# A decoder layer on one core: 432 transfers of ScalarE's results issued from ScalarE's queue instead of SyncE's

## The chip, the core and the metric

The kernel runs on one core of a Trainium2 chip. The core has five engines with a queue of instructions each: TensorE (PE in the profile; its weight loads are PEld), VectorE (DVE), ScalarE (ACT), GpSimd (POOL) and SyncE (SP). SP does no arithmetic here: its queue only issues DMA transfers. Each queue is worked off in order, and a transfer can be issued from SP's, ACT's or POOL's. The metric is the device time of one execution in microseconds (us); shorter is better.

## What is computed

The reference is one decoder layer on x of shape 8 x 512 x 512 (batch, position, feature) in float32, with a context of the same shape:

```python
x = layernorm(x + mamba(x))                  # L0_attn
x = layernorm(x + attention(x, ctx, mask))   # L0_xattn, 16 heads of 32
x = layernorm(x + ffn(x))                    # 32 experts, 4 per token, plus a shared one
```

`mamba` normalizes x, projects it to 1024 inner channels and 1024 gates, convolves over 4 positions, and derives dt, B and C from the result (`x_dbl = x_main @ x_proj_w`, split into 32 + 16 + 16 columns). For each channel and each of 16 states it runs `h = exp(A*dt)*h + dt*B*x` along the positions and sums `h*C` over the states. `attention` is a softmax of q·k over 512 context positions. `ffn` picks four experts for each token by a gate, with a capacity of 640 tokens for each expert.

## The kernel before

The program has three functions in a row: `layers` (mamba, attention, the gate and the shared expert), `experts`, and `finish` (the last layer norm). The change touches `layers` alone.

`layers` handles 16 chunks of mamba: 8 batch elements in two chunks of 256 positions. Each chunk has 32 steps: 4 groups of 256 channels (q), 4 groups of states (g) and two halves (jj). In a step ACT makes four decays with `exp` (`decays`, L480) and copies the carried state into the head of a tile (`carry`, L488). DVE multiplies dt·x with B (`steps_in`, L494), runs the scan (L501) and multiplies with C (`collect`, L510). PE then sums over the states (L521). The decays have two buffers, so those of one step are written while the scan before runs.

While the mamba of batch element b runs, its steps are filled up with pieces of the attention of element b-1 and with the keys and values of element b (`sources`, `units`). The attention of the last element runs by itself after the last chunk. The work around the change is:

- **B and C.** `x_proj` makes dt, B and C on PE; `spill` copies them to `xd` on ACT (L406) and stores B and C to DRAM (L408). `bcast` (L418) reads them back, repeated over the partitions. Once for each chunk.
- **Values.** `values` projects the context on PE; `put` copies the rows to `v` on ACT (L721) and stores them (L722); `units` reads them back much later (L765). Four times for each batch element.
- **Maxima.** For a pair of heads, `maximum` computes scores on PE (L813), which DVE reduces to `mx` (L815). `negate` turns them around on PE (L822), ACT negates them into `nm` (L826), and two transfers put one row each into the query tile `qa` (L829). `weigh` (L839) multiplies keys with this tile, so that the scores come out less their maximum, and ACT takes `exp` of them (L843).
- **Result and sums.** `gather` (L855) multiplies the values with these exponentials. `split` copies the finished pair to `raw` on ACT (L867); four transfers put its halves into `attT` (L875) and the sums into `total` (L876). After two pairs, `divide` takes the reciprocal on ACT (L888, L889) and finishes it on DVE (L892 to L894). `total` has one buffer, so the next pair's sums can be written only when L894 has read it.

Further ACT operations on whose results DVE works at once are the chain of `prepare` (L447 to L453, then DVE L457 to L460), the first tap of the convolution (L369, then L377) and the roots of the layer norms (L68, L69, then L73).

SP's queue also issues all loads of weights and activations, the repeated dt and dt·x (`repeat`, L428) and the tiles of the attention (`spread`, L799 to L803). Two things set the order of a queue. The steps' code places a part of the side work in each third of a step and holds the second half of many a part back by three thirds (`wait`, `settle`). Then a planner, when the program is built, orders each engine's queue by when it expects an instruction to be ready: the order on an engine is not quite that of the source. Its waits follow from the data.

Of the kernel before, what the change touches and what calls it, by code (L numbers as in the profile page):

```python
# [17 lines left out]
P = 128  # L18
# [6 lines left out]
NST = 16  # L25
RANK = 32
# [10 lines left out]
HD = 32  # L37
# [51 lines left out]
def layers(ctx, tc, a, x1d, filld, based, xbuf):  # L89
# [23 lines left out]
    nc = tc.nc  # L113
# [23 lines left out]
    def rows(w):  # L137
        return w.rearrange("(c p) f -> p c f", p=P)
# [108 lines left out]
    def quad(tag, name):  # L247
        return big(tag, name)[:, 0 : DC * S].rearrange("p (c t) -> p c t", c=DC)
# [148 lines left out]
    def x_proj(f):  # L397
        psd = psm.tile([P, 2, T], F32, tag="mm", name="ps_d")
        for c in range(CC):
            nc.tensor.matmul(  # L400
                psd[0:64, 0, :], w_x[:, c, :], f["xs"][c // 2][:, c % 2, :], start=(c == 0), stop=(c == CC - 1)
            )

        def spill():
            f["xd"] = xd = mp.tile([64, T], F32, tag="xd", name="xd")
            nc.scalar.copy(xd, psd[0:64, 0, :])  # L406
            f["scr"] = scr = dp.tile([2 * NST, T], F32, tag="scr", name="scr")
            nc.sync.dma_start(scr, xd[RANK : RANK + 2 * NST, :])  # L408

        return spill  # L410

# [160 lines left out]
    def load(name):  # L572
        loaded[name] = w = p2.tile([P, DC, D], F32, tag="wa", name="wa")
        nc.sync.dma_start(w, rows(a[name]))
# [124 lines left out]
    kept = {}  # L699

    def sources(b):

        st, todo = {}, []

        def begin():
            load("Wv")
            st["cT"] = cT = quad("s2", "cT")
            nc.sync.dma_start(cT, rows(a["ctx"][b]))
            st["mk"] = mk = p1.tile([P, S], U8, tag="mk", name="mk")
            nc.sync.dma_start(mk, a["mask"][b : b + 1, :].to_broadcast([P, S]))  # L710
            kept[b] = [dp.tile([S, D], F32, tag="vd", name="vd"), dp.tile([D, S], F32, tag="kd", name="kd")]

        def values(pc):
            if pc == 0:
                load("Wk")
            w, cT = loaded["Wv"], st["cT"]
            ps = dense(lambda dc: cT[:, dc, pc * P : (pc + 1) * P], lambda dc: w[:, dc, :])

            def put():
                v = p3.tile([P, D], F32, tag="row", name="v")  # L720
                nc.scalar.copy(v, ps)  # L721
                nc.sync.dma_start(kept[b][0][pc * P : (pc + 1) * P, :], v)  # L722

            return put

        def keys(oc):
            if oc == 0 and b:
                load("Wq")
            w, cT = loaded["Wk"], st["cT"]
            ps = dense(lambda dc: w[:, dc, oc * P : (oc + 1) * P], lambda dc: cT[:, dc, :])  # L730

            def put():

                k = p3.tile([P, D], F32, tag="row", name="k")
                nc.vector.scalar_tensor_tensor(k, ps, bk[:, oc : oc + 1], st["mk"], ALU.add, ALU.mult)
                nc.sync.dma_start(kept[b][1][oc * P : (oc + 1) * P, :], k)

            return put

        todo.append((0, begin, False))  # L740
        for j in range(SC):
            todo.append((3.4, lambda j=j: values(j), False))
        for j in range(DC):
            todo.append((3.4, lambda j=j: keys(j), False))
        return todo

    def dense(lhs, rhs):
        ps = psm.tile([P, S], F32, tag="mm", name="ps_p")
        for dc in range(DC):
            nc.tensor.matmul(ps, lhs(dc), rhs(dc), start=(dc == 0), stop=(dc == DC - 1))  # L750
        return ps

    def units(b):

        st = {}
# [61 lines left out]
        def negate(i):  # L817

            mx = st.pop(("mx", i))
            pm = psm.tile([P, S], F32, tag="mm", name="ps_m")  # L820
            for lt in range(SC):
                nc.tensor.transpose(pm[0:2, lt * P : (lt + 1) * P], mx[:, lt, :], ident)  # L822

            def put():
                nm = p3.tile([P, D], F32, tag="row", name="nm")
                nc.scalar.mul(nm[0:2, :], pm[0:2, :], -1.0)  # L826
                for j in range(2):
                    r0 = j * 2 * HD + HD + 1
                    nc.sync.dma_start(st[i][0][r0 : r0 + 1, :], nm[j : j + 1, :])  # L829

            return put

# [14 lines left out]
        def gather(i, kc):  # L847

            if kc == 0:
                st["po"] = pso.tile([P, S], F32, tag="po", name="po")  # L850
                if i == 0:
                    st["attT"] = quad("s2", "attT")
            po, eT = st["po"], st.pop(("eT", i, kc))
            for j in range(2):
                nc.tensor.matmul(  # L855
                    po[j * 2 * HD : (j + 1) * 2 * HD, :],
                    va[:, kc, i, j * HD : (j + 2) * HD],
                    eT[:, j, :],
                    start=(kc == 0),
                    stop=(kc == SC - 1),  # L860
                )
            if kc < SC - 1:
                return

            def split():
                raw = p3.tile([P, D], F32, tag="row", name="raw")
                nc.scalar.copy(raw, po)  # L867
                if i % 2 == 0:
                    st["total"] = p1.tile([P, S], F32, tag="total", name="total")
                attT, total, oc = st["attT"], st["total"], i // 2  # L870
                for j in range(2):

                    r0, r1 = (0, HD) if j == 0 else (3 * HD, 2 * HD)
                    to = slice((i % 2) * 2 * HD + j * HD, (i % 2) * 2 * HD + (j + 1) * HD)
                    nc.sync.dma_start(attT[to, oc, :], raw[r0 : r0 + HD, :])  # L875
                    nc.sync.dma_start(total[to, :], raw[r1 : r1 + HD, :])  # L876

            return split

# [114 lines left out]
        for n in range(pairs * SC + 4):  # L994
            i, k = n // SC, n % SC
# [568 lines left out]
```

## Time and profile before

| | us |
|---|---|
| median of three runs (5405.52 to 5409.17) | 5408.32 |
| the profiled execution | 5406.28 |
| its span, first to last instruction | 5404.6 |
| PE busy | 4672.4 (86%) |
| DVE busy | 4235.9 (78%) |
| ACT busy | 2593.6 (48%) |
| stretch with mamba and attention together, 405 to 3515 us: PE / DVE / ACT busy | 2620.7 / 2836.3 / 1831.4 |
| the last attention by itself, 3515 to 3840 us: PE / DVE / ACT busy | 283.1 / 130.8 / 82.3 |
| experts and last norm, 3840 to 5404.6 us: PE / DVE / ACT busy | 1493.5 / 904.3 / 442.6 |

Times in the profile count from the span's start. "L480" is line 480 of the kernel. In a list of operations, `out<-in` names what is written and read, and "x4" counts instructions. Brackets give the idle time of the engine just before, and what ended it. In a list of waits, "DVE m L73 <- ACT r L69: 33.5, 26, 3.3" says that DVE's operation on line 73 stood waiting for ACT's line 69 for 33.5 us in total, 26 times, 3.3 us at the longest. "SPq" and "ACTq" mark instructions that only issue a transfer; they do not count as busy time. An operation's slack is the time between its end and the start of the operation that uses its result.

### The profile page before, as it was taken

To read this page: it belongs to the slowest core of one execution; us is meant where nothing else is said; L and a number is where in the kernel's file an instruction comes from. 1 tells how busy PE (TensorE), PEld (TensorE's weight loads), DVE (VectorE), ACT (ScalarE), POOL (GpSimd) and SP (SyncE) were. 2 spreads that over 40 slices of the span, in tenths; PEclk is the share of its full clock that TensorE was granted. 3 is DMA by queue.
4 is the path that set the end of the run, shared out by engine and by line. 5 is a ranking of instruction groups with operands and counts; after the bars stand their busy time and mean duration, and the time that the engine had idled before them with its cause. 6 is when DMAs were issued, how large, how long until landed. Compare 5 with 4: busy or idle time off the path is not lost. (4 is left out here: it accounts for less than half of the span.)

```text
span 5404.6 us, 53991 instructions
## 1 busy us (share of the span) xinstructions
PE 4672.4 (86%) x17320; PEld 2476.6 (46%) x17320; DVE 4235.9 (78%) x5369; ACT 2593.6 (48%) x5726; POOL 570.3 (11%) x426
## 2 busy tenths in 40 slices
PE   6768889788888988988888888789999999999994
PEld 3324234234333423433333342333677777777773
DVE  7999899989989989898998998943566555665554
ACT  5566565565656556566565655523222222222223
POOL 1000002002000200200200020011111111111111
PEclk8879989999999999999999999899999999999997
DMA  8875346345444634634544463342344444544544
GB/s 236 266 224 146 87 96 208 81 114 176 114 104 117 197 77 109 189 98 107 174 125 100 117 200 78 91 146 66 103 128 127 123 117 118 127 127 121 129 115 144
DMA packets 486427, 719.03 MB, mean 133 GB/s; under 512 B 117137, under 2 KB 200625, under 8 KB 484096
## 3 DMA queue, kind: packets, MB, share of 16 engines
q1 hardware_dynamic: 450128, 627.16, 41.1%
q0 software_dynamic: 33280, 76.90, 7.5%
q10 hardware_dynamic: 2736, 11.54, 0.5%
q8 instruction: 137, 2.24, 0.2%
q14 instruction: 146, 1.20, 0.1%
HBM read 391.24 MB, written 165.05 MB: 103 GB/s over the span
## 5 line engine op out<-in xcount | busy, mean ns | idle before, releaser
L480 ACT ACTIVATE l_da<-rep,l_aneg 128x256 f32<-128x256 f32 x2048 | 895.0, 501 | 941.8 <-DVE h L501 877.0
L501 DVE TENSOR_TENSOR_SCAN h<-l_da,h 128x1028 f32<-128x1028 f32 x512 | 1166.0, 2292 | 20.3 <-ACT l_da L480 17.7
L494 DVE TENSOR_TENSOR h<-rep,bc 128x1024 f32<-128x1024 f32 x512 | 614.7, 1218 | 103.1 <-PE py L521 84.6
L510 DVE TENSOR_TENSOR h<-h,bc 128x1024 f32<-128x1024 f32 x512 | 619.5, 1217 | 2.1
L521 PE MATMUL py<-h,l_fold 128*32 128x512 f32 x2048 | 368.3, 644 | 113.4 <-DVE h L510 96.5
L813 PE MATMUL ps_s<-l_ka,l_qa 64*128 64x512 f32 x1024 | 325.6, 707 | 137.8 <-DVE mx L815 137.6
L1314 PE MATMUL ps_h<-xT,w 128*128 128x320 f32 x1536 | 435.8, 433 | 0.0
L1394 POOL DMA_INDIRECT based<-y,xe x160 | 255.5, 1597 | 1309.9 <-ACT y L1417 630.0
L1335 DVE TENSOR_TENSOR hT<-ps_h,p 128x320 f32<-128x320 f32 x128 | 62.9, 492 | 378.5 <-PE ps_h L1314 378.5
L815 DVE TENSOR_REDUCE mx<-ps_s 128x2 f32<-128x1024 f32 x256 | 310.2, 1217 | 58.5 <-PE ps_s L813 58.3
L1314 PEld LDWEIGHTS ps_h<-xT,w 128*128 128x128 f32 x1536 | 292.5, 191 | 118.3 <-issue 0.4
L855 PE MATMUL po<-eT,l_va 128*64 128x512 f32 x1024 | 301.5, 670 | 47.6 <-ACT eT L843 43.1
L839 PE MATMUL ps_t<-l_qa,l_ka 64*128 64x512 f32 x1024 | 308.4, 674 | 23.8 <-ACT eT L843 23.1
L843 ACT ACTIVATE eT<-ps_t 128x1024 f32<-128x1024 f32 x256 | 259.0, 1015 | 128.8 <-PE ps_t L839 128.5
L688 POOL DMA_INDIRECT xbuf<-x2t,dest x128 | 217.2, 1697 | 860.4 <-DVE dest L679 760.8
L1314 PE MATMUL ps_h<-t,s 128*128 128x320 f32 x1024 | 286.1, 432 | 0.0
L343 PE MATMUL ps_z<-xnT,wm 128*128 128x256 f32 x1024 | 238.0, 388 | 30.0 <-DVE o L561 24.3
L750 PE MATMUL ps_p<-x2T,wa 128*128 128x512 f32 x512 | 241.5, 626 | 18.1 <-ACT hT L944 10.4
L552 PE MATMUL po<-wm,zs 128*128 128x512 f32 x512 | 244.7, 632 | 13.8 <-DVE z L957 11.9
L343 PE MATMUL ps_x<-xnT,wm 128*128 128x256 f32 x1024 | 246.5, 393 | 4.5 <-ACT xnT L332 2.5
L343 PEld LDWEIGHTS ps_z<-xnT,wm 128*128 128x128 f32 x1024 | 194.6, 193 | 93.0 <-DVE o L561 37.5
L343 PEld LDWEIGHTS ps_x<-xnT,wm 128*128 128x128 f32 x1024 | 196.1, 195 | 80.5 <-issue 43.8
(232 smaller groups left out, 7170.4 us busy)
## 6 DMA issues: line engine op xcount, KB each, us to landing
w<-in_w SPq DMA_DIRECT2D x93, 1024.0 KB
wm<-in_in_proj_w SPq DMA_DIRECT2D x128, 512.0 KB
rep<-dt SPq DMA_DIRECT2D x256, 256.0 KB
rep<-dtx SPq DMA_DIRECT2D x256, 256.0 KB
xbuf<-zero SPq DMA_DIRECT2D x32, 1362.5 KB
xe<-xbuf SPq DMA_DIRECT2D x32, 1362.5 KB
wm<-in_out_proj_w SPq DMA_DIRECT2D x64, 512.0 KB
wa<-in_sw SPq DMA_DIRECT2D x24, 1024.0 KB
```

The lines of the kernel that those rows point to most:

```text
L343: nc.tensor.matmul(ps[:, i, :], w[:, dc, i * P : (i + 1) * P], f["xnT"][:, dc, :], start=(dc == 0), stop=(dc == DC - 1),)
L480: nc.scalar.activation(da[:, n, 1:], dt[:, j, i, :], AF.Exp, scale=aneg[:, 2 * q + i, 2 * jj + j, g : g + 1])
L494: nc.vector.tensor_tensor(h[:, :, 1:], dtx.rearrange("p j i t -> p (j i) t"), f["bc", g][0], ALU.mult)
L501: nc.vector.tensor_tensor_scan(flat, da.rearrange("p n t -> p (n t)"), flat, 0.0, ALU.mult, ALU.add)
L510: nc.vector.tensor_tensor(h[:, :, 0:T], h[:, :, 1:], f["bc", g][1], ALU.mult)
L521: nc.tensor.matmul(f["py"][j * QP : (j + 1) * QP, :, :], fold, hs[j // 2][:, 2 * (j % 2) : 2 * (j % 2) + 2, 0:T], start=False, stop=g == N ...
L813: nc.tensor.matmul(ps[:, j, :], qa[r, lt * P : (lt + 1) * P], ka[r, :], start=True, stop=True)
L815: return lambda: nc.vector.tensor_reduce(mx[:, lt, :].unsqueeze(2), ps, AX.X, ALU.max) and None
L839: nc.tensor.matmul(ps[:, j, :], ka[r, kc * P : (kc + 1) * P], qa[r, :], start=True, stop=True)
L843: nc.scalar.activation(eT, ps, AF.Exp)
L855: nc.tensor.matmul(po[j * 2 * HD : (j + 1) * 2 * HD, :], va[:, kc, i, j * HD : (j + 2) * HD], eT[:, j, :], start=(kc == 0), stop=(kc == SC ...
L1314: nc.tensor.matmul(ps, w[:, n, r * P : (r + 1) * P], x[:, n, :], start=not more and n == 0, stop=n == 1, skip_group_check=more,)
```

## The change

In five lines the issuing queue changes from SP's to ACT's. What is transferred, and what each transfer has to wait for, stays the same.

```diff
             nc.scalar.copy(xd, psd[0:64, 0, :])
             f["scr"] = scr = dp.tile([2 * NST, T], F32, tag="scr", name="scr")
-            nc.sync.dma_start(scr, xd[RANK : RANK + 2 * NST, :])
+            nc.scalar.dma_start(scr, xd[RANK : RANK + 2 * NST, :])
...
                 nc.scalar.copy(v, ps)
-                nc.sync.dma_start(kept[b][0][pc * P : (pc + 1) * P, :], v)
+                nc.scalar.dma_start(kept[b][0][pc * P : (pc + 1) * P, :], v)
...
                 for j in range(2):
                     r0 = j * 2 * HD + HD + 1
-                    nc.sync.dma_start(st[i][0][r0 : r0 + 1, :], nm[j : j + 1, :])
+                    nc.scalar.dma_start(st[i][0][r0 : r0 + 1, :], nm[j : j + 1, :])
...
                     to = slice((i % 2) * 2 * HD + j * HD, (i % 2) * 2 * HD + (j + 1) * HD)
-                    nc.sync.dma_start(attT[to, oc, :], raw[r0 : r0 + HD, :])
-                    nc.sync.dma_start(total[to, :], raw[r1 : r1 + HD, :])
+                    nc.scalar.dma_start(attT[to, oc, :], raw[r0 : r0 + HD, :])
+                    nc.scalar.dma_start(total[to, :], raw[r1 : r1 + HD, :])
```

## The prediction, as put on record

> **What bounds the kernel.** I read the page's totals and slices first, then the busy times by stage, then what each engine waits for in the long stage, then the timelines around the moved transfers. The slices show two regimes: up to about 3515 us VectorE (DVE) is nearly full and ScalarE (ACT) half full; from 3840 us on TensorE (PE) is full. All moved transfers lie in the first regime and in the short piece between the two, so the expert stage (1564.6 us) is left alone. This is the stage of 3110 us, as one row of busy times (PE, PEld, DVE, ACT, POOL), and what DVE, then ACT, waits for in it (us in total, times, longest):
>
> ```profile
> 405.00:3515.00 3110.00, 2620.65 (x9447) 1121.79 (x9447) 2836.32 (x3063) 1831.35 (x4088) 252.14 (x179) 0.93 0.47 126
> ...
> DVE h L494 <- PE py L521: 84.6, 35, 5.4
> DVE m L73 <- ACT r L69: 33.5, 26, 3.3
> DVE dtx L457 <- ACT dtx L453: 30.2, 23, 3.1
> DVE xs L377 <- ACT xs L369: 27.0, 14, 4.1
> DVE h L501 <- ACT l_da L480: 17.7, 7, 2.8
> ...
> DVE h L494 <- DMA rep<-dtx: 6.5, 6, 1.6
> DVE xr L913 <- DMA xr<-x1d: 6.3, 6, 1.2
> ...
> ACT l_da L480 <- DVE h L501: 818.1, 338, 7.7
> ...
> ACT l_da L480 <- DMA rep<-dt: 46.9, 31, 5.0
> ```
>
> To be seen: DVE is busy 2836.3 of 3110 us (91%), so this stage ends when DVE's chain ends. ACT is busy 59% and stands idle 818 us ahead of a scan: there a few us more cost nothing. But DVE also stands on ACT's heels, in short chains: L73, L457, L377, L501. A delay of ACT there is a delay of DVE. For transfers DVE waits little: 6.5 + 6.3 + 2.7 (xt) + 1.7 (wm) = 17.2 us in the whole stage.
>
> **The change part by part.** Five lines move 16 + 32 + 128 + 256 = 432 transfers from SP's queue to ACT's. Nothing is added or left out. Their issue times on SP (min/median/max, ns):
>
> ```profile
> L875 SPq DMA_DIRECT2D attT<-raw x128: 507/582/1280, 564.8 to 3705.4; - x128
> L876 SPq DMA_DIRECT2D total<-raw x128: 507/588/1793, 565.4 to 3706.1; - x128
> L829 SPq DMA_DIRECT2D l_qa<-nm x128: 497/553/1807, 531.6 to 3690.0; - x128
> ```
>
> L408 takes 317 ns x16 and L722 339 ns x32 by the same view. So 16x0.317 + 32x0.339 + 128x0.553 + 128x0.582 + 128x0.588 = 5.1 + 10.8 + 70.8 + 74.5 + 75.3 = 236.5 us of issuing leave SP and enter ACT. Per pair of heads that is one burst of four behind `raw` (2 x (0.582 + 0.588) = 2.34 us) and one of two behind `nm` (1.11 us). 56 of the 64 pairs run in the long stage: 56 x 3.45 = 193 us, 6% of ACT's time there.
>
> No such transfer is on ACT's queue before the change, so its price there is bounded: the nearest ACT rows are the stores of the result (338 ns, 8 times; SP's stores of this kind, L959, take 329 ns) and three weight loads (441 ns; SP's 368). I take SP's own durations, since shape and destination are the same. What an issue holds up shows at the end of the kernel:
>
> ```profile
> 5368.65 0.19 ACT L1493 ACTIVATE r<-v 128x4 f32<-128x4 f32 x1
> 5368.78 0.37 ACTq L1507 DMA_DIRECT2D out<-o  x1
> 5369.19 0.21 ACT L1494 ACTIVATE r<-r 128x4 f32<-128x4 f32 x1 [0.35 <-ACT r L1493]
> ...
> 5372.33 0.81 ACT L1506 ACTIVATE o<-acc,m,r 128x512 f32<-128x512 f32 x1
> 5372.34 0.36 ACTq L1507 DMA_DIRECT2D out<-o  x1
> 5373.05 0.19 ACT L1494 ACTIVATE r<-r 128x4 f32<-128x4 f32 x1
> ```
>
> Behind a short operation the issue leaves ACT idle for 0.35 us; under a long one it costs nothing. In both, the planner put another ready operation between the producer and the transfer. So I take one issue of each burst as covered by the operation in flight and the rest as delay: 1.76 us behind `raw`, 0.55 us behind `nm`.
>
> *Where the delay reaches DVE.* A delay travels down ACT's queue until an idle gap eats it. At 1038.17 `raw` is followed by 2.91 us of idle time: the burst fits, cost 0. At 1081.92 it does not:
>
> ```profile
> 1081.92 0.57 ACT L867 COPY raw<-po 128x512 f32<-128x512 f32 x1
> ...
> 1085.05 0.61 ACT L453 ACTIVATE dtx<-u 128x512 f32<-128x512 f32 x1
> ...
> 1085.70 0.69 DVE L457 SCALAR_TENSOR_TENSOR dtx<-dtx,u 128x512 f32<-128x512 f32 x1 [0.67 <-ACT dtx L453]
> ```
>
> Six ACT operations run without a gap from `raw` to L453, and DVE already waits for L453: the whole delay is DVE's. I followed all bursts of one batch (about 980 to 1210 us; the pattern repeats in the seven batches) like this, a delay less the consumer's slack, with whole bursts: 0.63 (scan at 1004.25), 0.54 (scan at 1023.15), 2.27 (L457 at 1085.70), 2.68 (L73 at 1148.48, behind `raw` and `nm` together), 1.07 (L377 at 1176.71), 1.38 (L892 at 1187.11), 2.16 (scan at 1205.03) = 10.7 us, x7 = 75 us. That is the upper end. With one issue of each burst covered: about 0.1 + 0 + 1.7 + 1.55 + 0.5 + 0.8 + 1.6 = 6.2 us, x7 = 44 us. DVE also waits for PE about 120 us in the stage (84.6 and six smaller rows); a late DVE finds PE's results ready, so part comes back. I have no row for the share and take half, between none and all: **+22 us** (0 to 75).
>
> *The lone attention of the last batch* (3515 to 3840 us): PE works without a gap, one key chunk in 2.9 us, and ACT has 1.4 to 2.0 us idle in each. A burst of 2.34 us pushes the next `eT` by about 1 us, which the next L855 can take; only where `nm` and the reciprocals (L888, L889) follow too is PE held, some 0.85 us in four places: **+3 us** (0 to 8). The first 405 us hold four values and two B/C transfers: 0.
>
> *What SP wins.* SP's waits in these lines (L408 241.9, L829 124.1, L722 77.2, L875 51.7 us) are SP standing ready early: most of these transfers go out 0.03 us after their data. Behind them stand loads that mostly wait for data of their own. Of all engine waits on a transfer, only the `rep<-dt` pairs once a batch (593.97 and 596.61 us and their like) have moved transfers just ahead of them, 14 waits of about 0.85 us, all on ACT and none on DVE: **0** on the path (gain at most 17.2 us, all of DVE's waits on transfers). The pieces of `raw` land 2.0 us after their issue (median, by the semaphores' updates in the trace); nobody but L888 (5.7 us in 4 times) waits for that.
>
> *Added waits.* On ACT the `total` transfer waits for L894, which still reads the tile: pair 6 of each batch has SP hold it 4.65 us behind `raw`. In ACT's queue everything behind it (decays, `eT`) would wait too. SP's order there shows both `attT` transfers issued ahead of both `total` transfers, so the planner sees this wait coming; I take 0, upper end 7 x 4.65 = 33 us. Each transfer also waits for the landing of the eighth one before it (eight landing semaphores in rotation); those had landed before `raw` or `nm` ended in all but six cases, 5.2 us in all, and one of 8.6 us behind `v` at 208 us: 0.
>
> Two rules of the Trainium skill weigh this. "DMA: Bandwidth & Descriptors", section "Issuing engines are not separate DMA queues", says that issuing from several engines saves only the sequencer's time for initiating transfers, usually little beside the transfer itself. By that rule the gain is near 0, as priced above, since the time saved is SP's. "Advanced Engine Details and Errata", section "Sequencer Loop", says that other engine instructions can be read and queued while the sequencer executes a control instruction. If that held for these issues, they would cost ACT nothing and the sum would be 0; the row of 5369.19 above, idle for 0.35 us right behind an issue of 0.37 us, speaks against it.
>
> **Sum.** 22 + 3 + 0 + 0 = +25 us on the profiled execution's 5406.3 us: 5431 us. The median of the runs, 5408.3, lies 2.0 us above that execution; carried over: **5433 us**. About 0.2%, 10.8 us, is what a measurement of this kernel can tell from no change.
>
> **Rivals.**
> - *Covered* (chance 0.27): ACT's 818 us of idle time ahead of the scans swallow the bursts, because the plan is made anew with the transfers in it. For: 59% load. Against: seven places in a batch with no gap. It gives 5408 to 5414, say 5410; within 0.2%.
> - *SP relieved* (0.17), the other sign: loads of `rep`, `xr`, `xt` and `wm` no longer stand behind blocked transfers in SP's queue and DVE's 17.2 us vanish, plus ACT's 46.9 us wherever DVE follows: 5408 - 17 = 5391. It decides once ACT's exposed delay is under 6 us in total, i.e. under 1 us per batch, so that the net gain passes 10.8 us. Against: of the moved transfers only those 14 ACT waits stand behind.
> - *A wait taken over by ACT* (0.13): L876 behind L894, or a landing semaphore of a late SP load, holds ACT's queue: 33 us of it, and the bursts wholly exposed: 5408 + 3 + 22 to 75 + 33, say 5466 and up to 5519.
>
> **Numbers.** Forecast (5419 to 5450) 0.43; the rivals as above. Faster 0.17, same 0.27, slower 0.43 + 0.13 = 0.56. The range reaches from the middle of the gain case to the taken-over wait: 5392 to 5472; what is left out is about 0.11 below and 0.07 above.
>
> **What would show it.** Right: DVE busy time in the stage unchanged, its rows on L453, L69, L369 and L480 larger by some 20 us together, the ACT queue with 432 more issues of 0.55 to 0.59 us, SP with as many fewer. Wrong: those rows unchanged (covered); issues on ACT under 0.3 us; DVE's and ACT's waits on `rep`, `xr`, `o` smaller and the time with them (SP relieved); a new row of ACT waiting for L894 or for landings. Since the plan is made at build time, a reordering elsewhere on ACT or PE could outweigh all these terms.

## The result, and the profile after

The changed kernel takes 5446.9 us (median of four runs, 5444.19 to 5457.02) where the kernel before, run beside it, takes 5407.5 (5405.52 to 5409.17): a ratio of 1.0076, 95% interval 1.0059 to 1.0094. It is slower by about 41 us; 25 were forecast. Its profiled execution took 5445.4 us, its span 5443.6.

Where the 39.0 us between the two spans come from, cut at the first scan of the third chunk, the end of the last scan and TensorE's first instruction on L1285, where the experts begin to transpose their tokens:

| us | before | after | difference |
|---|---|---|---|
| to the third chunk's first scan | 396.2 | 399.2 | +3.0 |
| from there to the end of the last scan | 3125.8 | 3155.1 | +29.3 |
| to the experts' L1285 | 262.2 | 267.8 | +5.6 |
| to the end | 1620.4 | 1621.4 | +1.0 |

The long stage by its busy times (PE, PEld, DVE, ACT, POOL), the row that answers to that of 405 to 3515 us before:

```profile
408.00:3547.00 3139.00, 2665.07 (x9474) 1123.81 (x9472) 2842.03 (x3070) 1836.18 (x4088) 259.49 (x179) 0.92 0.46 125
```

DVE's busy time moved by 5.7 us (2836.3 before), ACT's by 4.8; the stage got 29 us longer. So on DVE, which bounds the stage, it is waiting that grew. PE's busy time grew by 44.4 us, at a granted clock of 0.92 instead of 0.93 (the row's third number from the end); the account of the prediction comes back to this. What DVE waits for in this stage (us in total, times, longest):

```profile
DVE h L494 <- PE py L521: 86.2, 42, 3.9
DVE m L73 <- ACT r L69: 41.7, 31, 3.1
DVE dtx L457 <- ACT dtx L453: 40.6, 13, 4.2
DVE mx L815 <- PE ps_s L813: 40.5, 34, 3.7
DVE zs L535 <- PE py L521: 22.3, 7, 3.5
DVE h L494 <- DMA rep<-dtx: 15.5, 7, 2.4
...
DVE xs L377 <- ACT xs L369: 5.6, 9, 0.8
```

Two things are to be seen. L457 and L73 wait more, by 10.4 and 8.2 us. But L377 fell from 27.0 to 5.6, and the scan's wait for L480, 17.7 us before, is gone, so DVE's waits for ACT *fell* in sum, from 125 to 108 us. What grew most are waits for PE, from 120 to 152 us in sum: L815 from 14.0 to 40.5, L535 from 2.3 to 22.3. The wait of L494 for the repeated dt·x grew too, from 6.5 to 15.5. A mere delay of ACT in the old order would not make a wait for ACT vanish. The order of issue has changed on every engine but GpSimd: both programs have the same instructions, and TensorE's and VectorE's stand in another order.

What ACT waits for in the same stage:

```profile
ACT l_da L480 <- DVE h L501: 708.8, 296, 9.2
...
ACT eT L843 <- DMA total<-raw: 49.8, 18, 4.8
...
ACT l_da L480 <- DMA rep<-dt: 30.4, 12, 4.2
...
ACT r L68 <- DMA total<-raw: 22.3, 6, 3.9
...
ACT u L447 <- DMA total<-raw: 17.8, 7, 2.5
```

The rows "<- DMA total<-raw" are new: ACT stood behind its own issues. The issues on ACT's queue (min/median/max, ns):

```profile
L875 ACTq DMA_DIRECT2D attT<-raw x128: 514/554/1871, 570.5 to 3742.8; - x128
L876 ACTq DMA_DIRECT2D total<-raw x128: 514/603/1880, 571.1 to 3743.4; - x128
L829 ACTq DMA_DIRECT2D l_qa<-nm x128: 504/555/1762, 537.0 to 3725.3; - x128
```

All 432 issues together take 277.5 us, and for 209 us of this no ACT operation is in flight.

### The profile page after: what moved, and what is told of

Same layout as the page of the kernel before. It is cut to its first block, busy times and chain, and to the rows that moved or that the text cites. A ratio compares the mean times of both kernels' runs of the same rounds, so it can differ in the third digit from the quotient of the medians.

```text
span 5443.6 us, 53861 instructions
## 1 busy us (share of the span) xinstructions
PE 4716.5 (87%) x17320; PEld 2477.4 (46%) x17320; DVE 4240.5 (78%) x5369; ACT 2594.8 (48%) x5726; POOL 578.7 (11%) x426
## 5 line engine op out<-in xcount | busy, mean ns | idle before, releaser
L480 ACT ACTIVATE l_da<-rep,l_aneg 128x256 f32<-128x256 f32 x2048 | 906.4, 501 | 848.3 <-DVE h L501 766.8
L494 DVE TENSOR_TENSOR h<-rep,bc 128x1024 f32<-128x1024 f32 x512 | 614.6, 1219 | 114.7 <-PE py L521 86.2
L521 PE MATMUL py<-h,l_fold 128*32 128x512 f32 x2048 | 412.3, 659 | 201.2 <-DVE h L510 181.5
L813 PE MATMUL ps_s<-l_ka,l_qa 64*128 64x512 f32 x1024 | 321.4, 700 | 117.1 <-DVE mx L815 116.0
L815 DVE TENSOR_REDUCE mx<-ps_s 128x2 f32<-128x1024 f32 x256 | 310.7, 1218 | 85.5 <-PE ps_s L813 85.3
L839 PE MATMUL ps_t<-l_qa,l_ka 64*128 64x512 f32 x1024 | 311.1, 673 | 25.9 <-ACT eT L843 25.0
L521 PEld LDWEIGHTS py<-h,l_fold 128*32 128x32 f32 x2048 | 58.6, 112 | 433.2 <-issue 214.2
```

Of the source, the lines that this page charges most:

```text
L480: nc.scalar.activation(da[:, n, 1:], dt[:, j, i, :], AF.Exp, scale=aneg[:, 2 * q + i, 2 * jj + j, g : g + 1])
L494: nc.vector.tensor_tensor(h[:, :, 1:], dtx.rearrange("p j i t -> p (j i) t"), f["bc", g][0], ALU.mult)
L521: nc.tensor.matmul(f["py"][j * QP : (j + 1) * QP, :, :], fold, hs[j // 2][:, 2 * (j % 2) : 2 * (j % 2) + 2, 0:T], start=False, stop=g == N ...
L813: nc.tensor.matmul(ps[:, j, :], qa[r, lt * P : (lt + 1) * P], ka[r, :], start=True, stop=True)
L815: return lambda: nc.vector.tensor_reduce(mx[:, lt, :].unsqueeze(2), ps, AX.X, ALU.max) and None
L839: nc.tensor.matmul(ps[:, j, :], ka[r, kc * P : (kc + 1) * P], qa[r, :], start=True, stop=True)
```

## The experiments

Theories. **1, issue time:** the issues hold ACT, and the delay reaches DVE. **2, the plan:** the planner makes another order for the new queue, and the order is the worse one. **3, transfers in the way:** landing waits, and issues that take long beside SyncE's traffic, hold ACT.

In all kernels below the five lines read the queue from a table, `getattr(nc, Q["nm"]).dma_start(...)`, so that an assignment is one line. Where an order is *held*, the program is traced twice. The first trace, with another assignment, gives each engine's planned order; in the second, edges that only fix the order of issue tie each instruction to the one before it on its engine. An instruction that is on another engine in the first trace (a moved transfer) is left to the planner:

```python
for name, engine in plan:            # the order of the other assignment
    i = traced.get(name)
    if i is None or i.engine != engine:
        continue
    if engine in last:
        tc.add_manual_dep(i, last[engine], ...)   # NoSync: order of issue, no wait
    last[engine] = name
```

All results (ratios to the kernel before, run on the same chip, with 95% intervals; "cost" is the ratio less 1, times 5406 us, and its interval reaches some 5 to 10 us to either side; a difference of two costs is uncertain by about 10):

| order held | issued from ScalarE | median us | ratio | cost us |
|---|---|---|---|---|
| before's | all 432 | 5502.7 | 1.0174 (1.0161 to 1.0187) | +94 |
| before's | raw, 256 | 5477.3 | 1.0130 (1.0115 to 1.0146) | +70 |
| before's | none; copies in their place | 5470.7 | 1.0121 (1.0106 to 1.0137) | +65 |
| the change's | none | 5428.5 | 1.0041 (1.0026 to 1.0057) | +22 |
| (the change) | all 432 | 5446.9 | 1.0076 (1.0059 to 1.0094) | +41 |
| raw's | none | 5370.5 | 0.9935 (0.9921 to 0.9948) | -35 |
| raw's | scr, vd, 48 | 5374.3 | 0.9944 (0.9931 to 0.9958) | -30 |
| (its own) | raw, 256 | 5408.6 | 1.0005 (0.9996 to 1.0014) | +3 |
| (its own) | nm, 128 | 5409.8 | 1.0014 (1.0002 to 1.0025) | +8 |
| (its own) | raw and nm, 384 | 5448.6 | 1.0075 (1.0061 to 1.0089) | +41 |
| (its own) | scr, vd, 48 | 5392.4 | 0.9974 (0.9964 to 0.9984) | -14 |
| scr, vd's | none | 5389.9 | 0.9973 (0.9964 to 0.9982) | -15 |
| (its own) | none; all 432 from GpSimd | 5414.9 | 1.0020 (1.0011 to 1.0029) | +11 |

### The change's order with all transfers on SyncE

```diff
-Q = dict(scr="scalar", vd="scalar", nm="scalar", attT="scalar", total="scalar")
+Q = dict(scr="sync", vd="sync", nm="sync", attT="sync", total="sync")
...
+            hold(tc, plan)    # plan: all five on "scalar"
```

> All 432 transfers stay on SyncE's queue, as before, but TensorE, VectorE, GpSimd and every ScalarE operation are issued in the changed kernel's order (edges in the plan that fix the order of issue and wait for nothing); only the place of the 432 on SyncE is left to the planner. Theory 1 (issue time: the 432 issues hold ScalarE, and the delay reaches VectorE): the cost goes with the queue, so the time returns to the kernel before, 5400 to 5415 us, and VectorE's idle time in the long stage to about 274 us. Theory 2 (the plan: the order that the planner made for the new queue is the worse one, whoever issues): it keeps the changed kernel's time, 5438 to 5455 us. Theory 3 (landing waits: transfers stand behind the eighth transfer before them, now of two queues at once): 5400 to 5415 us as in theory 1; the next run and the single groups part the two.

Measured: 5428.5 us, +22, between the two forecasts. Neither theory alone. ACT issues none of the 432 here, and yet about half of the loss stays: the order costs 22 us by itself, the issues in this order 41 - 22 = 19. DVE's largest waits in this kernel's long stage (400 to 3544 us), close to those of the change, but for L73's (41.7 there):

```profile
DVE h L494 <- PE py L521: 83.9, 45, 3.9
DVE mx L815 <- PE ps_s L813: 52.7, 30, 4.9
DVE dtx L457 <- ACT dtx L453: 43.9, 13, 4.2
DVE m L73 <- ACT r L69: 28.2, 25, 3.9
DVE zs L535 <- PE py L521: 17.9, 6, 3.1
```

### The order before with all transfers on ScalarE

```diff
 Q = dict(scr="scalar", vd="scalar", nm="scalar", attT="scalar", total="scalar")
...
+            hold(tc, plan)    # plan: all five on "sync"
```

> All 432 transfers go out from ScalarE's queue, as in the change, but TensorE, VectorE, GpSimd and every ScalarE operation are issued in the order of the kernel before; the place of the 432 on ScalarE is left to the planner, which puts most of them directly behind their producer or one or two operations later. Theory 1 (issue time): at least the changed kernel's time, 5440 to 5470 us, since the order is not adapted to issues that now hold ScalarE; VectorE's idle time in the long stage about 300 us. Theory 2 (the plan): the time of the kernel before, 5395 to 5415 us. If the two share the cost, both held orders lie about half way, near 5425 us.

Measured: 5502.7 us, +94, above all that was expected. Theory 2 alone falls: this is the old order, and it is the slowest of all. So the new order, bad by itself, is better than the old one once the issues are on ACT: it saves 53 us. DVE's waits in this kernel's long stage (407 to 3607 us):

```profile
DVE h L494 <- PE py L521: 102.1, 38, 6.7
DVE m L73 <- ACT r L69: 49.6, 32, 3.2
DVE dtx L457 <- ACT dtx L453: 49.2, 25, 3.5
DVE xs L377 <- ACT xs L369: 30.2, 21, 3.9
DVE h L501 <- ACT l_da L480: 22.4, 7, 5.4
...
DVE total L892 <- ACT r L889: 14.3, 8, 3.1
```

Here all rows on ACT grew, at the places that the prediction had walked through: L457 from 30.2 to 49.2, L73 from 33.5 to 49.6, L892 from 2.3 to 14.3. The waits for ACT rose from 125 to 189 us, those for PE from 120 to 146. The prediction's example, in a timeline:

```profile
1100.97 0.57 ACT L867 COPY raw<-po 128x512 f32<-128x512 f32 x1
...
1101.57 0.54 ACTq L875 DMA_DIRECT2D attT<-raw  x1
1102.14 0.60 ACTq L876 DMA_DIRECT2D total<-raw  x1
...
1102.79 0.60 ACTq L875 DMA_DIRECT2D attT<-raw  x1
1103.43 0.60 ACTq L876 DMA_DIRECT2D total<-raw  x1
1104.08 0.47 ACT L447 ACTIVATE u<-ps_dt,l_b_dt 128x256 f32<-128x256 f32 x1 [2.54 <-DMA total<-raw]
...
1107.38 0.69 DVE L457 SCALAR_TENSOR_TENSOR dtx<-dtx,u 128x512 f32<-128x512 f32 x1 [3.53 <-ACT dtx L453]
```

ACT idles 2.54 us, the whole burst with no issue covered, and L457's wait is 3.53 us instead of 0.67. In the changed kernel, where L453 comes no earlier behind `raw` (6.5 us after its start, 5.8 here, 3.1 before), the planner lets DVE do three other things first:

```profile
1099.48 1.22 DVE L494 TENSOR_TENSOR h<-rep,bc 128x1024 f32<-128x1024 f32 x1 [3.91 <-PE py L521]
1100.63 0.68 DVE L535 TENSOR_TENSOR zs<-zs,py 128x512 f32<-128x512 f32 x1
1101.22 1.22 DVE L815 TENSOR_REDUCE mx<-ps_s 128x2 f32<-128x1024 f32 x1
1102.36 0.68 DVE L457 SCALAR_TENSOR_TENSOR dtx<-dtx,u 128x512 f32<-128x512 f32 x1
```

L457 waits for nothing. The wait has moved to L494, and from ACT to PE. PE takes as long here as before (from L813 to L521 6.16 us, before 6.11); before, DVE had L457 to L460 to do meanwhile. This is how a plan trades one wait for the other. It is not what makes this order a bad one: the fastest kernel below has the same wait at this place (3.90 us).

### Plain copies in the place of the issues

Is it ACT's time, or something about the transfers? This kernel keeps all 432 on SyncE, holds the order before, and gives ACT copies that nobody reads where the kernel above had the issues (two for each of raw and nm, one for each of scr and vd; one of the five lines is shown):

```diff
-Q = dict(scr="scalar", vd="scalar", nm="scalar", attT="scalar", total="scalar")
+Q = dict(scr="sync", vd="sync", nm="sync", attT="sync", total="sync")
...
-                    getattr(nc, Q["attT"]).dma_start(attT[to, oc, :], raw[r0 : r0 + HD, :])
+                    getattr(nc, Q["attT"]).dma_start(attT[to, oc, :], raw[r0 : r0 + HD, :]); pad(nc, "attT", 2)
...
+            hold(tc, plan)    # plan: before's order, pads where the issues were
```

> All 432 transfers on SyncE's queue and every engine in the order of the kernel before; ScalarE gets plain copies that nobody reads where order_before_on_act had the transfers: two of 128x150 for each of the 384 out of raw and nm, one for each of the 48 of scr and vd. By the rows of ScalarE's copies (194 ns for 128x4, 576 for 128x512) one is about 305 ns, in all some 249 us, where that kernel's issues took 284 us, 219 of them in ScalarE's idle time. No transfer leaves ScalarE's queue, so no landing wait and no collision of two queues can hold it. Theory 1 (the time on ScalarE is the cost): most of that kernel's 96 us comes back, 5470 to 5505 us. Theory 3 (landing waits and long issues beside SyncE's transfers are the cost): 5406 to 5430 us.

Measured: 5470.7 us, +65. The same place:

```profile
1083.86 0.57 ACT L867 COPY raw<-po 128x512 f32<-128x512 f32 x1
1084.33 0.67 ACT L1539 CAST pad_attT<-pad_in 128x150 uint8<-128x150 f32 x2
...
1086.04 0.66 ACT L1539 CAST pad_total<-pad_in 128x150 uint8<-128x150 f32 x2
...
1086.60 0.47 ACT L447 ACTIVATE u<-ps_dt,l_b_dt 128x256 f32<-128x256 f32 x1
...
1089.90 0.69 DVE L457 SCALAR_TENSOR_TENSOR dtx<-dtx,u 128x512 f32<-128x512 f32 x1 [3.21 <-ACT dtx L453]
```

No transfer leaves ACT's queue, ACT is busy 2.17 us (1084.43 to 1086.60) instead of idle for 2.54, and L457 waits 3.21 us. So time on ACT's queue at these places is shown to cost 65 us by itself, about 0.7 of the 94. The other 29 (uncertain by some 11) go with what the copies (257 us in sum, for 284 of issues) do not imitate: 50 of that kernel's issues are over 0.8 us long and take 73.5 us, some 44 more than 50 issues of 0.58, while a copy takes 0.32 on the mean. Waits for landings can be little of it: ahead of an issue, ScalarE's queue stands still for about 7 us in that whole kernel. TensorE's granted clock differs as well (0.927 there, 0.932 with the copies). Theory 3 has about these 29 us at most; how they divide, the runs do not tell.

### One group alone

```diff
-Q = dict(scr="scalar", vd="scalar", nm="scalar", attT="scalar", total="scalar")
+Q = dict(scr="sync", vd="sync", nm="sync", attT="scalar", total="scalar")
```

> Only attention's result and sums (the 256 transfers out of raw, L875 and L876) go out from ScalarE's queue; scr, vd and the negated maxima stay on SyncE. Theory 1 (issue time): the cost goes by issue time on ScalarE: this group has about 181 of the 277 us that the 432 issues took, so 0.65 of the 39 us, 5425 to 5440 us. Theory 3 (landing waits, with the long stalls beside SyncE's transfers): by the long issues, this group has about 50 of 79 us, much the same. Theory 2 (the plan): no rule by group; TensorE's and VectorE's orders change here nearly as much as in the whole change, so again near 5440 us. It serves for the sum of the parts.

> Only the negated maxima (128 transfers, L829) go out from ScalarE's queue. Theory 1 (issue time): about 74 of 277 us of issue, so 0.25 of 39 us, 5412 to 5424 us. Theory 2 (the plan): TensorE's order changes here by 84 lines where the whole change has 484, and VectorE's by 194 where it has 1789, so near the kernel before, 5405 to 5412 us.

> Only scr and vd (48 transfers, L408 and L722) go out from ScalarE's queue. raw alone came to 5408.6 us and nm alone to 5409.8, so if the groups add up, these 48 must carry the rest of the 40 us: 5435 to 5447 us. If the groups do not add up (theory 2, the plan: each assignment makes the planner find another order, good or bad by some 20 us, and the sum of issue times says nothing), these 48 with 20 us of issue, of which 5 lay in idle time of ScalarE, stay within 5400 to 5415 us.

> 384 of the 432 (raw and nm) go out from ScalarE's queue, scr and vd from SyncE's. Its orders on TensorE and VectorE are closer to the changed kernel's (177 and 281 lines of difference) than to those of the kernel before (302 and 1498). Adding up (raw +2, nm +3): 5409 to 5416 us. Theory 1 in its plain form (cost by issue time on ScalarE, 255 of 277 us): 5438 to 5446 us. Theory 2 (an order like the changed kernel's costs its 22 us, the issues 18 more): 5435 to 5445 us.

Measured: +3 (raw), +8 (nm), -14 (scr and vd, faster than either forecast), +41 (raw and nm). The groups do not add up, and a cost by the sum of issue times is refuted in this plain form: raw alone holds ACT for 185 us and costs nothing that can be told, while raw and nm together (264 us) cost all of it. I had expected 5425 to 5440 us for raw. What it was instead, the next two runs show.

### Raw's order, with and without its issues

```diff
-Q = dict(scr="scalar", vd="scalar", nm="scalar", attT="scalar", total="scalar")
+Q = dict(scr="sync", vd="sync", nm="sync", attT="sync", total="sync")
...
+            hold(tc, plan)    # plan: attT and total on "scalar"
```

> All 432 transfers on SyncE's queue, with TensorE, VectorE, GpSimd and ScalarE's operations held in the order that the planner made for raw on ScalarE. That kernel ran in 5408.6 us with 186 us of issues on ScalarE. If those issues cost as much as the change's (about 0.65 of 18 us, 12 us, or more) and its order is simply a better one, this kernel is faster than both, 5380 to 5400 us. If the issues are hidden there and the order is worth the same as before's, 5402 to 5412 us.

Measured: 5370.5 us, -35, the fastest of all and 10 us below the range expected: faster than both kernels, with the queues of the kernel before. So raw's issues do cost, 38 us, and a better order hid that. DVE's waits in its long stage (404 to 3479 us):

```profile
DVE h L494 <- PE py L521: 82.9, 37, 4.3
DVE mx L815 <- PE ps_s L813: 40.3, 20, 5.5
DVE dtx L457 <- ACT dtx L453: 24.9, 13, 3.1
DVE m L73 <- ACT r L69: 14.7, 19, 1.4
...
DVE xs L377 <- ACT xs L369: 6.4, 10, 1.8
```

Its waits for ACT are half of before's, 64 us for 125; those for PE are higher, 150 for 120. One reading: a plan made for an ACT that loses time leaves room behind ACT's results, and where ACT then does not lose it, the room is gain. It is not shown, and it is not enough: the change's order on SyncE was made in the same way, has 92 us of waits for ACT and 160 for PE, and is 22 us slower than before.

The counterpart, before's order with raw on ScalarE:

```diff
-Q = dict(scr="scalar", vd="scalar", nm="scalar", attT="scalar", total="scalar")
+Q = dict(scr="sync", vd="sync", nm="sync", attT="scalar", total="scalar")
...
+            hold(tc, plan)    # plan: all five on "sync"
```

> The 256 transfers out of raw on ScalarE's queue, the rest on SyncE's, all engines held in the order of the kernel before. In the planner's own order the same assignment came to 5408.6 us, 38 above the same order with all on SyncE. Theory 1 (cost by issue time, in an order that is not adapted): 186 of the 284 us of issues that cost 96 us, so 63 us, 5455 to 5480 us. Theory 2 (the plan alone): 5400 to 5412 us.

Measured: 5477.3 us, +70, as theory 1 expected. The same 256 issues cost 70 us in an order made without them and 38 in one made with them.

### Scr and vd: order or queue

```diff
 Q = dict(scr="sync", vd="sync", nm="sync", attT="sync", total="sync")
...
+            hold(tc, plan)    # plan: scr and vd on "scalar"
```

> All 432 transfers on SyncE's queue, in the order that the planner made for scr and vd on ScalarE (5392.4 us there, 10 to 14 below the kernel before). If that gain is the plan's: 5380 to 5395 us, as low or a little lower. If it is the queue's (scr and vd no longer stand behind others on SyncE, so bc lands earlier): back at 5400 to 5410 us.

```diff
-Q = dict(scr="sync", vd="sync", nm="sync", attT="sync", total="sync")
+Q = dict(scr="scalar", vd="scalar", nm="sync", attT="sync", total="sync")
...
+            hold(tc, plan)    # plan: attT and total on "scalar"
```

> The fastest order so far (that made for raw on ScalarE, 5370.5 us with all on SyncE), with scr and vd alone on ScalarE's queue. If moving these 48 gains by itself, 5358 to 5366 us, the fastest of all; if their 17 us of issues, of which 4.4 lay in idle time, cost nothing, 5368 to 5374 us; if they cost as the others do (0.2 us per us of issue), 5372 to 5378 us.

Measured: the order alone gives 0.9973, with the queue 0.9974; and in raw's order these 48 on ScalarE give 0.9944 beside 0.9935 without, which the intervals do not part. The gain of scr and vd is the plan's. Their issues cost nothing that can be measured: of 16 us, 3 to 5 lie in idle time of ACT.

### All transfers from GpSimd

```diff
-Q = dict(scr="scalar", vd="scalar", nm="scalar", attT="scalar", total="scalar")
+Q = dict(scr="gpsimd", vd="gpsimd", nm="gpsimd", attT="gpsimd", total="gpsimd")
```

> All 432 transfers go out from GpSimd's queue. ScalarE issues none of them, SyncE is relieved of them as in the change, and TensorE's order differs from before by 11 lines, VectorE's by none. If SyncE's queue had cost the kernel before anything (my rival of the relieved SyncE), this gains up to 17 us: 5388 to 5402 us. If nothing is to be had from SyncE, 5402 to 5410 us. If GpSimd's issues are slow or disturb VectorE, slower than 5415 us. In no case do ScalarE's waits for raw and nm's place in its stream return, so 5440 us and more would speak against theory 1.

Measured: 5414.9 us, +11, at the edge of the forecast for slow issues. SyncE is as free here as in the change, ACT is not held, VectorE's order is the same as before's, and TensorE's and ScalarE's differ in a few places. The time gains nothing, and ACT's waits for transfers in the long stage (405 to 3530 us) are no shorter (46.9 and 31.3 before):

```profile
ACT l_da L480 <- DMA rep<-dt: 45.9, 25, 4.6
ACT o L540 <- DMA o<-in_x: 35.5, 7, 6.1
```

DVE's waits for transfers did fall, from 17.2 to 10.8 us, so a gain of some 6 us may be hidden in the +11. Why it is slower by 0.2% stays open. Late landings do not explain it: the transfers out of raw land 2.0 (`attT`) and 2.2 us (`total`) after their issue (median), SyncE's took 2.0.

## Why the prediction was right, and where its steps were not

The time came out 14 us above the forecast, inside its range and on its side. That the size came out is luck. The way there holds in part only, and two errors cancel: the issues, in the order that it had before it, cost 94 us and not 25, and the plan's answer to them, -53 us, was left out. What held is the mechanism of the sign: issues on ACT delay DVE through short chains.

- **Issue durations.** 236.5 us were forecast from medians; 277.5 were measured. SyncE's own 432 issues before add up to 271.2 us: the medians had left out 51 issues of over 0.8 us, and these came along. The row's maxima (1280, 1793, 1807 ns) had shown them.
- **"One issue of each burst covered by the operation in flight"** took too much off. It is a quarter of the issue time behind `raw` and half of that behind `nm`; in the held order 14% (26 of 184 us) and 32% (26 of 82) were covered, and in the example ACT idles for the whole burst, 2.54 us. "Advanced Engine Details and Errata" of the Trainium skill, section "Sequencer Loop", lets other instructions be read and queued meanwhile. In the held order an operation starts during an issue in 13 of 432 cases, each right behind another operation; an idle ACT starts none before the issue ends, so the prediction was right to side with the row.
- **"Part comes back from PE, take half"** failed for the unchanged order: DVE's waits for PE did not shrink there, they grew by 26 us. The upper end of the walk, 75 us with whole bursts, came nearer: DVE's waits for ACT rose by 64 us, and the stage by 90.
- **Which places.** In the held order L457 (+19.0 for 15.9 by the walk's 7 x 2.27), L73 (+16.1 for 18.8) and L892 (+12.0 for 9.7) came near to the walk. The scans (+12.7 for 23.3: 4.7 behind L480 and 8.0 behind L488) and L377 (+3.2 for 7.5) did not.
- **The plan** was the step that was missing. It stood in the last sentence as something that "could outweigh all these terms", without a price. It is worth -53 us here: 94 in the old order, 41 in the new. So +22 for the long stage met the measured +29 not because half of a delay is absorbed, but because an order made for it moved DVE's and PE's work.
- **The signs named in advance.** L453, L69, L369 and L480 were to grow by some 20 us together; they fell by 20.5 (+10.4 + 8.2 - 21.4 - 17.7). DVE's busy time stayed, as said, and ACT has its 432 issues.
- **Lone attention:** +5.6 for +3, inside 0 to 8. In the held order it is +10.2, outside. **First 405 us:** +3.0 for 0. With the change's order and no issue on ACT they are longer by 3.6, but with the order before and the issues on ACT by 2.4, so the runs do not tell what it is. **Experts:** +1.0, left alone as said.
- **SyncE's gain** was put at 0 and is none (all on GpSimd). That agrees with "DMA: Bandwidth & Descriptors" of the Trainium skill, section "Issuing engines are not separate DMA queues": only issue time is saved. Here the time did not gain by SyncE's 271 us of it.
- **Added waits** at 0 was too low for the change. The planner saw L894 coming, as said (14 of 128 `total` transfers stand 7 to 10 operations behind their `raw`, and one wait of 3.4 us for L894 is left). But in the changed kernel ACT's queue stands still ahead of an issue for about 27 us, 12.2 of them in six waits of 2.0 to 2.1 us that L829's issue spends on the landing of a `rep<-dtx` of SyncE's. These can be part of the 19 us that the issues cost in this order; how much of them reaches DVE, no run tells. In the held order it is about 7 us.

Of the rivals, the covered one is out (94 us in the old order), and so is the relieved SyncE as a gain in time. The wait taken over by ACT came in part: about 27 us of standing still on ACT's queue in the change, where the rival had 33.

What stays open is why one order is better than another by up to 57 us (raw's to the change's, all on SyncE). DVE's waits for ACT (64 and 92 us), for PE (150 and 160) and for transfers (14 and 21) tell them apart; which of the planner's choices does it, no run here tells. One thing changes with the order that no run holds fixed: TensorE's granted clock. Its mean was 0.934 to 0.938 in the runs of raw's order on SyncE and 0.923 to 0.929 in those of the change's; it was 0.925 to 0.929 in the order before with all issues on ScalarE, and 0.931 to 0.940 in all runs of the kernel before. At half clock a matmul takes nearly twice as long. In the changed kernel four of L839 take 1.92 us at 1094.09, and 1.02 at 1100.34 (the clock is the third number from the end):

```profile
1094.09:1096.01 1.92, 1.92 (x8) 0.41 (x6) 1.22 (x1) 0.44 (x2) 0.00 (x0) 0.50 0.42 102
1100.34:1101.36 1.02, 1.02 (x8) 0.26 (x6) 1.02 (x3) 0.23 (x1) 0.00 (x0) 1.00 0.02 2
```

So a part of DVE's longer waits for PE may come by way of the clock. Whether the lower clock makes these waits or follows from them, the runs do not part. It is not the whole: the copies cost 65 us at 0.932 to 0.936.

## What to carry to other kernels

Moving a transfer to a computing engine's queue costs that engine the issue, and where a chain of its operations feeds the bottleneck the whole burst is delay: follow each burst to its consumer, take means rather than medians for the issues, and count no cover that no row shows. If a planner orders the program, an edit to a queue is also a new order everywhere, here worth between -35 and +22 us by itself, of the size of what the issues cost in orders made for them (0 to 38): hold the order once with the edit and once without it before giving a reason for either. And try such orders for themselves; the best kernel of this study has the old queues and an order that was planned for something else.

## What the runs showed that I had not expected

- An issue from SBUF to SBUF is 0.5 to 0.6 us on any of the queues (medians: 0.50 on GpSimd, 0.55 to 0.59 on SyncE, 0.55 to 0.60 on ScalarE). But about one in nine of the 432 takes 0.8 to 1.9 us, on SyncE before (51) and on ScalarE after (48), and none does on GpSimd, where the longest takes 0.75. Of the 48, 32 overlap an issue of SyncE's for `rep` or `bc`, and of the other 384 issues 106 overlap one of SyncE's; before, with one queue, none of the 51 could, so that the overlap is not the only cause.
- The cost of an issue on ScalarE depends on the order around it more than on its length: raw's 185 us cost 70 us in one order and 38 in another, while scr's and vd's 16 us cost nothing.
